# Earlier transposes in the first and the fourth slot of a decoder layer's schedule

## The chip, the cores and the metric

The kernel runs on one core of a Trainium2 chip. The metric is the device time of one execution in microseconds. TensorE (PE in the profile) multiplies matrices and transposes, VectorE (DVE) and ScalarE (ACT) work on elements, GpSimd (POOL) does element work in SBUF only, SyncE (SP) issues DMAs. Matmul results land in PSUM, which has eight banks.

## The reference, cut to what matters

One decoder layer on x of 32 batches, 256 tokens, 256 features, in float32: self attention with 16 query heads and 4 key/value heads of size 64 (rotary positions, a linear position bias), cross attention to a context of the same size with 16 heads of size 16 in windows of 64 with a mask by cell, and a gated feed-forward of 1024 features with quantized weights and activations. After each, the residual is added and a layer norm follows.

```python
x = _layernorm(x + self_attention(x))             # 16 heads, softmax over all 256 keys
x = _layernorm(x + cross_attention(x, ctx, cell)) # own layer norms, windows, mask, softmax
x = _layernorm(x + feed_forward(x))               # down(silu(gate(x)) * up(x)), quantized
```

## The kernel before, in words

All 32 batches go through one software pipeline. Time is cut into **slots**; four slots make a **round** (`m, part = divmod(slot, 4)`), and a batch takes four rounds, sixteen slots. In each round one quarter of a batch's self attention and one quarter of another batch's cross attention are worked on; cross attention runs four rounds behind (`k = m - CROSS`).

A self-attention round has two units. For each unit `self_scores` (L392 on TensorE) makes scores in two PSUM banks `s`, and VectorE adds the position bias and takes each row's maximum, `nm` (L408). `self_exp` (L426, ScalarE) takes the exponentials, two for each half, and their sums. `self_turn` transposes them (`t`, L453) and ScalarE copies them to SBUF as `pT` (L458). In the next round `self_values` multiplies by v (`o`, L470) and ScalarE copies the result to `oT` (L477). `self_inverse` takes the reciprocals of the sums and spreads them (L439, L441, VectorE); `self_spread` transposes them into bank `R` (L485); `self_normal` multiplies `oT` by `R` (L493, VectorE).

A cross-attention round has one unit: `cross_scores` (`xs`, L662, four banks; maxima `xnm` L676 on VectorE), `cross_exp` (L692), `cross_turn` (`xt`, L701; ScalarE copies to `xpT`, L703), `cross_values` (`xo`, L717; copy `xoT`, L726) and `cross_back` (`xr`, L737; `on`, L743).

All else is written as generators with `yield n` for "go on n slots later", and one call `parts()` per slot runs those that are due: `self_inputs` (projections `proj` L329, `psin` L338, `v`, the addition `qT` L353 on GpSimd after a turned copy by DMA), `self_output` (`wo` L501, residual L511 to L528, `zqT` and `zT` L203/L204, `xq` L538, `qb` L556), `cross_inputs` (`zcT`, `xk` L610, `xv` L622, `xvaug` L630), `cross_output` (`zoT`, `xw` L763, L767) and `feed_forward` (`ff` L804 with a tanh L818 and a product L819 for the gate, L825 for up; `ffo` L851; the final norm's `y` and the store of the output). Some operations of ScalarE are kept in the list `last` and come at the end of the slot, in `flush()`.

What sets the order: TensorE, VectorE and ScalarE execute in exactly the order in which the slots record their instructions (`manual_schedule`). GpSimd and SyncE are ordered by the planner of the language, from the recorded program. All PSUM tiles come from one pool of eight banks that are handed out in turn, so a tile gets the bank of the tile eight allocations earlier and waits for its last reader:

```python
ps = ctx.enter_context(tc.tile_pool(name="ps", bufs=8, space=bass.MemoryType.PSUM))
```

Of the kernel before, what the change touches and what calls it, by code (L numbers as in the profile page):

```python
# [50 lines left out]
def kernel(  # L51
# [139 lines left out]
    def flush():  # L191
        while last:
            last.pop(0)()
# [694 lines left out]
    with tc.manual_schedule(engines={mybir.EngineType.PE, mybir.EngineType.DVE, mybir.EngineType.Activation}):  # L888
        running = []
        slot = min(starts)  # L890
        while starts or running:
            m, part = divmod(slot, 4)
            k = m - CROSS
            for gen in starts.pop(slot, ()):
                running.append([slot, gen])

            def cross(f, unit, *more):
                if 0 <= unit < 4 * B:
                    f(*divmod(unit, 4), *more)

            def pair(f, unit):
                if 0 <= unit < 4 * B:
                    f(*divmod(unit, 4))

            def own(f, unit, *more):
                if 0 <= unit < 8 * B:
                    f(*divmod(unit, 8), *more)

            def parts():
                for r in list(running):  # L910
                    if r[0] == slot:
                        wait = next(r[1], r)
                        if wait is r:
                            running.remove(r)
                        else:
                            r[0] += wait or 1

            if part == 0:
                own(self_scores, 2 * m)
                own(self_scores, 2 * m + 1)  # L920
                own(self_exp, 2 * m, 0)
                own(self_exp, 2 * m, 1)
                own(self_exp, 2 * m + 1, 0)
                pair(self_values, m - 1)
                own(self_exp, 2 * m + 1, 1)
                pair(self_spread, m - 1)
                parts()
                pair(self_normal, m - 1)
                cross(cross_turn, k - 1, 0)
                cross(cross_turn, k - 1, 1)  # L930
            elif part == 1:
                parts()
                cross(cross_scores, k)
                cross(cross_values, k - 1)
                cross(cross_exp, k, 0)
            elif part == 2:
                parts()
                cross(cross_exp, k, 1)
                own(self_turn, 2 * m)
                cross(cross_back, k - 1)  # L940
            else:
                pair(self_inverse, m)
                parts()
                own(self_turn, 2 * m + 1)
            flush()
            slot += 1

# [88 lines left out]
```

## Time and profile before

| | us |
|---|---|
| median of 3 runs | 2231.85 (2231.59 to 2232.89) |
| the profiled execution's own time | 2230.19 |
| its span | 2228.4 |
| TensorE busy | 2148.1 (96%) |
| VectorE busy | 1740.1 (78%) |
| ScalarE busy | 1678.0 (75%) |
| GpSimd busy | 1106.4 (50%) |
| mean granted clock of TensorE | 0.986 |

From 140 us to 2030 us every stretch of 70 us has TensorE busy for over 69 us at a granted clock of 1.00; the rest is a start of some 100 us and an end of some 130 us. How to read rows in order of time: start and length in us, engine, line, operation, written tile <- read tiles, their sizes, the number of instructions merged into the row, and in brackets how long the engine stood idle before it and who ended that. Matmuls are pipelined, so the length of a row of TensorE contains about 0.15 us that lie under the next row; the steps from start to start show the pace. In the list of waits the columns are the engine, what waited, for whom, and us in total, times, longest.

### The profile page before, as it was taken

The numbers are of one execution on the slowest core, as the hardware profiler recorded it, in microseconds if no ns is written. First come the engines' busy times: TensorE is split into PE (matmuls) and PEld (weight loads), VectorE is DVE, ScalarE is ACT, GpSimd is POOL, SyncE is SP. The second block draws the span as 40 slices with busy tenths as digits, with TensorE's granted clock in tenths as the row PEclk, the third lists the DMA queues.
The fourth block names the chain that finished last, engine by engine and source line by source line (L and its number), as shares of the span: only waits on it lengthen the run. The fifth ranks groups of instructions, "written<-read, shape, count | busy, mean of one in ns | idle before, by whom it ended". The sixth has DMA issues, their size and how long they took to land.

```text
span 2228.4 us, 55216 instructions
## 1 busy us (share of the span) xinstructions
PE 2148.1 (96%) x17828; PEld 1672.0 (75%) x17828; DVE 1740.1 (78%) x6949; ACT 1678.0 (75%) x4961; POOL 1106.4 (50%) x1849
## 2 busy tenths in 40 slices
PE   7899999999999999999999999999999999999974
PEld 5687777777777777777777777777777777777752
DVE  4777888878887877887877887887788887888775
ACT  2577778887778877778787777887877887777862
POOL 4344554545554545544545544545555445555442
PEclk8999999999999999999999999999999999999996
DMA  6322222222222223222222322222222222222111
GB/s 206 94 57 56 69 55 63 62 56 70 70 54 62 64 55 73 68 57 63 61 58 70 69 59 58 60 64 65 70 66 53 66 58 63 70 63 49 34 41 31
DMA packets 191424, 144.05 MB, mean 65 GB/s; under 512 B 107808, under 2 KB 160928, under 8 KB 191136
## 3 DMA queue, kind: packets, MB, share of 16 engines
q1 hardware_dynamic: 189440, 136.95, 24.6%
q8 instruction: 142, 2.33, 0.5%
q10 hardware_dynamic: 1696, 3.57, 0.4%
q14 instruction: 146, 1.20, 0.2%
HBM read 39.50 MB, written 8.39 MB: 21 GB/s over the span
## 4 chain that ended last, share of the span: by engine, by line
PE 72%; DVE 11%; ACT 9%; issue 3%; DMA 2%; POOL 1%; SPq 1%; ACTq 0%; DVEq 0%; POOLq 0%
PE wo L501 10%; PE o L470 9%; PE proj L329 8%; PE t L453 8%; PE s L392 6%; PE ff L804 5%; ACT p L426 4%; PE xt L701 4%; PE xo L717 3%; PE xq L538 3%; PE xs L662 3%; PE ffo L851 3%; PE R L485 3%; PE xk L610 3%; PE xw L763 2%
## 5 line engine op out<-in xcount | busy, mean ns | idle before, releaser
L426 ACT ACTIVATE p<-p,nm 128x256 f32<-128x256 f32 x1024 | 507.3, 497 | 89.5 <-DVE nm L408 89.5
L458 ACT COPY pT<-t 128x512 f32<-128x512 f32 x512 | 275.9, 597 | 149.0 <-PE t L453 148.3
L408 DVE CUSTOM_DVE_ANT_0 p<-s,alibi 128x256 f32<-128x256 f32 x1024 | 361.9, 417 | 5.0 <-PE s L392 4.9
L692 ACT ACTIVATE xp<-xp,xnm 128x128 f32<-128x128 f32 x1024 | 327.2, 397 | 25.7 <-DVE xnm L676 25.7
L676 DVE CUSTOM_DVE_ANT_0 xp<-xs,mask 128x128 f32<-128x128 f32 x1024 | 225.8, 286 | 82.4 <-PE xs L662 82.1
L453 PE MATMUL t<-ident,p 128*128 128x128 f32 x2048 | 266.8, 273 | 0.9 <-ACT p L426 0.9
L470 PE MATMUL o<-pT,v 128*64 128x256 f32 x2048 | 261.0, 386 | 3.9 <-ACT pT L458 0.9
L453 PEld LDWEIGHTS t<-ident,p 128*128 128x128 f32 x2048 | 238.0, 141 | 27.0 <-ACT p L426 2.6
L353 POOL TENSOR_TENSOR qT<-qT,other 128x512 f32<-128x512 f32 x128 | 163.8, 1279 | 188.4 <-DMA other<-psin 138.7
L392 PE MATMUL s<-kT,qT 64*128 64x256 f32 x2048 | 255.7, 389 | 0.0
L329 PE MATMUL proj<-xT,wq_sb 128*128 128x256 f32 x1024 | 246.4, 385 | 0.0
L501 PE MATMUL wo<-wo_sb,oT 128*128 128x256 f32 x1024 | 245.3, 383 | 0.0
L470 PEld LDWEIGHTS o<-pT,v 128*64 128x64 f32 x2048 | 144.3, 136 | 106.7 <-issue 21.2
L392 PEld LDWEIGHTS s<-kT,qT 64*128 64x128 f32 x2048 | 187.9, 186 | 38.0 <-issue 16.1
L501 PEld LDWEIGHTS wo<-wo_sb,oT 128*128 128x128 f32 x1024 | 191.5, 192 | 27.0 <-DVE gu L297 0.3
L329 PEld LDWEIGHTS proj<-xT,wq_sb 128*128 128x128 f32 x1024 | 188.1, 193 | 21.7
L426 ACT ACTIVATION_READ_ACCUMULATOR p<-p,nm 128x1 f32 x1024 | 192.4, 188 | 0.0
L493 DVE TENSOR_TENSOR oT<-oT,R 128x512 f32<-128x512 f32 x128 | 86.9, 679 | 114.2 <-ACT oT L477 104.2
L840 POOL TENSOR_SCALAR gu<-gu,ffhup 128x1024 f32<-128x1024 f32 x64 | 72.8, 1137 | 161.3 <-DVE ffhup L836 161.3
L819 DVE SCALAR_TENSOR_TENSOR gu<-gu,ff 128x512 f32<-128x512 f32 x128 | 82.5, 684 | 77.2 <-ACT gu L818 77.2
L726 ACT COPY xoT<-xo 128x256 f32<-128x256 f32 x128 | 47.6, 372 | 124.9 <-PE xo L717 123.3
L600 POOL TENSOR_SCALAR mask<-ck_i,cq_sb 64x128 f32<-64x128 f32 (+1 forms) x96 | 70.2, 731 | 141.3 <-DVE xnm L676 135.3
(148 smaller groups left out, 4579.9 us busy)
## 6 DMA issues: line engine op xcount, KB each, us to landing
other<-psin SPq DMA_DIRECT2D x640, 64.0 KB, 2.0
xT<-in_xt_dram SPq DMA_DIRECT2D x32, 256.0 KB, 2.7
xs<-in_x_dram SPq DMA_DIRECT2D x32, 256.0 KB, 2.7
cs<-in_ctx_dram SPq DMA_DIRECT2D x32, 256.0 KB, 2.9
other<-qb SPq DMA_DIRECT2D x64, 128.0 KB, 2.0
kTz<-tr SPq DMA_DIRECT2D x256, 32.0 KB, 2.0
other<-qb SPq DMA_DIRECT2D x128, 64.0 KB, 1.9
out_dram<-x SPq DMA_DIRECT2D x32, 256.0 KB, 2.3
```

What stands on the lines that cost most here:

```text
L329: nc.tensor.matmul(pq[:, c * L : (c + 1) * L], w[:, dc, c * P : (c + 1) * P], xT[:, dc, :], start=(dc == 0), stop=(dc == NDC - 1),)
L353: nc.gpsimd.tensor_tensor(d2, d2, other, ALU.add)
L392: nc.tensor.matmul(banks[half][:, rr * L : (rr + 1) * L], qT[rows_, rr, qc * P : (qc + 1) * P], kT[rows_, kc, :], start=(rr == 0), stop=(r ...
L408: nc.vector.tensor_tensor_reduce(p[:, cols], banks[half][:, cols], alibi[:, 2 * (4 * kc + 2 * rp + rr) + half, :], -0.125, 3.0e38, ALU.add ...
L426: nc.scalar.activation(p[:, cols], p[:, cols], AF.Exp, bias=nm[:, rr : rr + 1], scale=-1.0, accum_out=s["sums", i // 2][:, e : e + 1],)
L453: nc.tensor.transpose(pt[:, j * P : (j + 1) * P], p[half][:, rr * L + kk * P : rr * L + (kk + 1) * P], ident,)
L458: nc.scalar.copy(pT[half], pt)
L470: nc.tensor.matmul(po[half * HD : (half + 1) * HD, rp * L : (rp + 1) * L], s["v"][:, kk, (2 * kc + half) * HD : (2 * kc + half + 1) * HD], ...
L501: nc.tensor.matmul(py[:, 0:D], s["oT", qc, kc][:, r, :], wo_sb[:, 4 * kc + r, :], start=(kc == 0 and r == 0), stop=(kc == 1 and r == 3),)
L676: nc.vector.tensor_tensor_reduce(p[:, cols], banks[2 * half + j // 2][:, j % 2 * P : (j % 2 + 1) * P], s["mask"][:, qc, :], -1.0, 3.0e38, ...
L692: nc.scalar.activation(p[:, cols], p[:, cols], AF.Exp, bias=s["xnm", i][half][:, j : j + 1], scale=-1.0)
L804: nc.tensor.matmul(pg, xiT[:, t, dc, :], ff_w[name][:, dc, half * 512 : (half + 1) * 512], start=(dc == 0), stop=(dc == NDC - 1),)
```

## The change

In a round's first slot `self_spread` and both calls of `cross_turn` are recorded directly behind `self_values`, ahead of the last pair of exponentials (`self_exp(2m+1, 1)`), of the slot's parts and of `self_normal`. In its fourth slot the transposes of the second unit are recorded ahead of the slot's parts.

```diff
             if part == 0:
...
                 own(self_exp, 2 * m + 1, 0)
                 pair(self_values, m - 1)
+                pair(self_spread, m - 1)
+                cross(cross_turn, k - 1, 0)
+                cross(cross_turn, k - 1, 1)
                 own(self_exp, 2 * m + 1, 1)
-                pair(self_spread, m - 1)
                 parts()
                 pair(self_normal, m - 1)
-                cross(cross_turn, k - 1, 0)
-                cross(cross_turn, k - 1, 1)
...
             else:
                 pair(self_inverse, m)
+                own(self_turn, 2 * m + 1)
                 parts()
-                own(self_turn, 2 * m + 1)
             flush()
```

In the built program the instructions are the same in number and kind. On TensorE `xt` (8 transposes) stands directly behind `R`, ahead of `zqT`, `xw` and the other parts of the first slot; `t` of the second unit stands ahead of the fourth slot's parts (gate, up, projection, or projection and `xv`). On ScalarE the two `xpT` copies stand between `oT` and the last two exponentials, and the second pair of `pT` copies ahead of the fourth slot's parts. VectorE's order is unchanged. On SyncE's queue the store of the output moves from behind the DMA transposes of `xiT` to ahead of the four `psin` copies that precede these. On GpSimd the addition L528 moves ahead of three small operations of `rstd_zo`.

## The prediction

> **What bounds the kernel now.** I read the engine shares first, then TensorE's groups in order of time over one batch in mid-run, then ScalarE and VectorE in the same microseconds, then the waits.
>
> ```profile
> PE 2148.1 (96%) x17828; PEld 1672.0 (75%) x17828; DVE 1740.1 (78%) x6949; ACT 1678.0 (75%) x4961; POOL 1106.4 (50%) x1849
> ```
>
> TensorE sets the time, but "96% busy" hides its stalls, since a matmul that waits halfway through a group counts as a longer group. So I look at the step from the start of one group to the start of the next. A batch repeats every 66.4 us (the start of xo at 1004.01, and six batches on at 1402.48). It has four rounds, which I call A to D by where the scores s start: A at 995.64, B at 1009.85, C at 1025.02, D at 1040.19. TensorE in order of time:
>
> ```profile
> 1002.85 0.82 PE L662 MATMUL xs<-kTz,xqT 32*64 32x256 f32 x16
> 1004.01 0.91 PE L717 MATMUL xo<-xpT,xvaug 128*32 128x64 f32 x32 [0.34 <-ACT xpT L703]
> 1004.85 1.16 PE L538 MATMUL xq<-zT,xq_w 128*128 128x128 f32 x8
> ...
> 1009.85 2.00 PE L392 MATMUL s<-kT,qT 64*128 64x256 f32 x16
> 1011.96 2.33 PE L470 MATMUL o<-pT,v 128*64 128x256 f32 x16
> 1014.22 0.66 PE L485 MATMUL R<-ident,wide 128*128 128x128 f32 x4
> ...
> 1018.27 0.71 PE L662 MATMUL xs<-kTz,xqT 32*128 32x256 f32 x8
> 1018.91 0.65 PE L717 MATMUL xo<-xpT,xvaug 128*32 128x64 f32 x32
> ```
>
> Two steps are long. Place (a), round A: xs to xo takes 1.16 where the same shape takes 0.61 in round D (1051.09 to 1051.70), and xo to xq 0.84 where xo takes 0.58: 0.81 us lost. Place (b), the start of round B: s to o 2.11 instead of 1.93, o to R 2.26 instead of 1.88 (both from round C): 0.56 lost. All other steps of the batch are at their usual pace, so some 1.37 us per batch is all that a better order can win back. ScalarE in the same stretch:
>
> ```profile
> 1001.67 0.56 ACT L477 COPY oT<-o 128x512 f32<-128x512 f32 x1
> ...
> 1003.13 0.35 ACT L204 COPY zT<-zqT 128x256 f32<-128x256 f32 x1
> 1003.38 1.06 ACT L703 COPY xpT<-xt 128x512 f32<-128x512 f32 x2
> ...
> 1009.51 1.09 ACT L458 COPY pT<-t 128x512 f32<-128x512 f32 x2
> 1010.45 1.31 ACT L818 ACTIVATE gu<-ff,ffg 128x512 f32<-128x512 f32 x2
> 1011.60 1.12 ACT L458 COPY pT<-t 128x512 f32<-128x512 f32 x2
> 1012.94 0.51 ACT L426 ACTIVATE p<-p,nm 128x256 f32<-128x256 f32 x1 [0.22 <-DVE nm L408]
> ```
>
> ScalarE runs without a gap worth naming from 998.70 to 1012.7; there it, and not TensorE, paces the core. At (a) the two xpT copies end at 1004.44, and xo waits for both. At (b) two things are late: the second pair of pT copies, and a PSUM bank. The waits and VectorE's rows name the bank:
>
> ```profile
> PEld xo L717 <- ACT xpT L703: 44.5, 99, 1.5
> PEld o L470 <- DVE gu L819: 14.7, 29, 0.5
> 1011.22 1.28 DVE L819 SCALAR_TENSOR_TENSOR gu<-gu,ff 128x512 f32<-128x512 f32 x2 [0.50 <-ACT gu L818]
> 1012.42 0.42 DVE L408 CUSTOM_DVE_ANT_0 p<-s,alibi 128x256 f32<-128x256 f32 x1
> ```
>
> The eight banks go round in turn; o is the eighth bank after the first gate bank (gate, gate, t, t, four of s, o), so it starts when L819 has read that one (11.22 + 0.70 = 11.92, o at 11.96). There are 29 such waits: 29 times a gate is followed by a round of scores. (a) looks the same near 272, 538, 738 and 1402 us, each with a 0.33 to 0.34 gap.
>
> **The change, part by part.** No instruction is added or removed; only orders differ. The reciprocal transposes R (L485) were already directly behind o on TensorE: nothing moves there.
>
> *First slot, cross transposes.* On ScalarE the two xpT copies go ahead of the last two exponentials (L426). oT starts at 1001.67 and holds the engine 0.46 (next start 1002.13). The copies hold it 0.95 (1003.38 to 1004.33), so the second ends at about 1003.19; xo is due at 1002.85 + 0.61 = 1003.46 and no longer waits. But the exponentials (1.00, from 1002.13 to 1003.13) now stand ahead of the zT copy: 1003.09 + 1.00 + 0.35 = 1004.44. xq, due at 1003.46 + 0.58 = 1004.04, reads zT and starts about 1004.49 (0.05 behind, as xo was). Before: 1004.85. So the wait moves from xo to xq and of 0.81 only 0.36 is won. Rounds B and D have no zT there, and in C xq starts at 1033.46 against a zT at about 1032.65: nothing. The delayed exponentials are read two slots later by t, covered by 4 us.
>
> On TensorE xt (0.87) goes ahead of zqT or xw. In A zqT is ready (L526 ends 998.26). In D, xw ends 0.87 later, so L767 moves from 1045.55 to about 1046.4, ends its statistics near 1047.4, and L493 starts at 1047.67 anyway because of oT: covered, by 0.3 us.
>
> *Fourth slot, t ahead of the parts.* t (0.87) goes ahead of gate (A), up (B), a projection (C), projection and xv (D). A: pT copies precede the two tanh (L818). xoT can start 0.16 earlier, as xo ends earlier, so ScalarE's stream runs 0.16 ahead: pT(first) 1009.35, pT(second) 1010.30, tanh from 1011.25 to 1012.5. s would start at 1009.85 - 0.36 = 1009.49; its second bank is that of the first pT copy, which ends 9.35 + 0.59 = 9.94, while s wants it two matmuls in (9.73): 0.25 lost anew. s then ends 9.98 + 1.69 = 11.67. The bank of o is now that of the third pT copy (about 10.9) and the last pT is there at 11.4, so neither holds o: R at 11.67 + 1.88 = 13.55, before 14.22. **0.67 won per batch at this point**; I use 0.65.
>
> What does it put late? tanh and L819 come after pT, and VectorE does L819 ahead of the maxima of s (L408). The second tanh ends near 12.55 instead of 11.76, L819 near 13.3; the maxima start at about 13.24 instead of 12.42, 0.82 late. Exponentials 13.76, six at 0.495 to 16.73, oT to 17.29, L493 17.35 to 18.0, which frees the fourth bank of xs (R's). xs starts at 18.27 - 0.65 = 17.62 and asks for that bank 0.48 later, 18.10. Covered, with a tenth to spare; behind that each microsecond costs one. xo's two copies end at 17.19 + 0.95 + 0.10 = 18.24, and xo is due at 17.62 + 0.64 = 18.26: covered, only because they too now precede the exponentials. ScalarE's 1.23 us of idle at 1019.64 takes the rest.
>
> D: psin (L338) needs the projection, 0.87 later: 1057.71 + 0.87 + 1.73 + 0.16 = 1060.47, and VectorE, filled since wo, reaches it at 1060.75. xv's second half ends 1062.2, needed 1062.3. Cover 0.1 to 0.3. B: up needed by 1024.45, ready 1024.0 - 0.65. C: psin 1041.56, ready 1040.25.
>
> *Queues.* On SP the output store (0.53 to issue, 256 KB) passes the four psin copies, the two xvaug copies and the two xiT transposes. It waits for the second y on ScalarE, about 1060.4, so is issued by 61.0; the psin copies behind it start at 61.49 after L338. If y came later, psin would be late, then qT on POOL; POOL idles 4.67 us after that qT. On POOL the x1 bias add passes three short rstd_zo operations; its input is ready at 1061.1 and POOL gets there at 1064.6. Both nothing.
>
> *A rule.* The Trainium skill, "Perfetto Trace Analysis", Identifying Performance Opportunities, Optimization Strategy, says that a bubble repeated on the saturated engine can mean too few SBUF or PSUM buffers for the next tile. The change adds no bank, so by that rule (b) stays: 29 x 0.36 = 10 us won. The rows say that the bank lacks only because of who reads it last (L819 at 11.92 against a pT copy at about 10.9): I go by the rows.
>
> *Tail.* At 2138.80 o waits 0.87 for a pT behind two tanh, and xt (2152.77) stands behind a zqT that waited 2.67: about 1 us each at most, 1.5 taken (0 to 2.5). The first two batches have no gate: nothing.
>
> **Sum.** 29 x 0.65 = 18.9, + 1.5 = 20.4. The profiled execution took 2230.19 (span 2228.4): 2209.8. The median of the runs is 1.66 above it: 2211.5, so **2212 us**. About 0.2% (4.5 us) is what a measurement of this kernel can tell from no change.
>
> **Rivals.**
> *Half of it* (0.14). Only one of the places pays, through xq's wait on zT or the covers of a tenth eating the rest: 0.25 to 0.4 per batch, 7 to 12 us: 2222. For it: both new waits (zT, pT) are my own findings. Against: the xpT and pT copies do come 1.2 us earlier.
> *ScalarE is the bound, nothing moves* (0.09). Its work from 998.70 to 1012.7 is the same sum. Against: what TensorE needs from it is moved ahead of what it doesn't. 2232.
> *All of it* (0.05). zT and pT turn out in time: 29 x 1.37 = 40: 2192.
> *Slower* (0.14). The maxima of round B: the cover is a tenth. If they start at 1014.2 rather than 1013.24, L493 ends 0.96 later, xs stalls 0.9, more than the 0.65: 29 x 0.28 = 8: 2240. It decides from 1013.95 on. For it: VectorE and ScalarE hand over four times in a row there. Against: the tanh can't be later than one pair of copies, 0.95.
>
> **Chances and range.** The main case has 0.58, 2204 to 2219 alone. With half (0.14) and no change (0.09) the range 2204 to 2232 holds 0.81. Faster 0.58 + 0.14 + 0.05 = 0.77; same 0.09; slower 0.14.
>
> **What would show it.** Right: xs to xo 0.61, a new wait of xq for zT near 0.4, o at pace 1.88 with no wait on L819, the maxima of round B some 0.8 later against s than before. Wrong: xs in round B waiting for L493 or oT, s waiting for pT by over 0.3, psin late behind the projection.

## The result, and the profile after

| | us |
|---|---|
| kernel before, median of 4 runs | 2231.72 (2230.14 to 2232.89) |
| changed kernel, median of 4 runs | 2205.71 (2202.09 to 2208.47) |
| ratio, with its 95% interval | 0.9883 (0.9866 to 0.9900) |
| profiled execution: before, after | 2230.19, 2208.47 |

The change wins 26 us by the medians; 20 were forecast. Profile against profile it wins 21.7, and takes 2208.47 where the sum gave 2209.8. That is nearly exact for the profiled execution, which is the longest of the four runs, but in part by luck: two errors cancelled in it, as shown below.

The engine shares of the page after:

```profile
PE 2127.6 (96%) x17766; PEld 1658.8 (75%) x17828; DVE 1742.3 (79%) x6949; ACT 1660.3 (75%) x4961; POOL 1107.7 (50%) x1849
```

TensorE is still "96% busy", and its busy time fell with the span: the row of shares cannot show a stall that hides inside a group of matmuls. The order of time can show it. TensorE, changed kernel; the columns are start and length in us, engine, line, operation:

```profile
993.51 1.25 PE L662 MATMUL xs<-kTz,xqT 32*64 32x256 f32 x16
...
1000.81 2.10 PE L392 MATMUL s<-kT,qT 64*128 64x256 f32 x16
1002.85 1.95 PE L470 MATMUL o<-pT,v 128*64 128x256 f32 x16
1004.73 0.66 PE L485 MATMUL R<-ident,wide 128*128 128x128 f32 x4
...
1008.78 0.71 PE L662 MATMUL xs<-kTz,xqT 32*128 32x256 f32 x8
1009.42 0.65 PE L717 MATMUL xo<-xpT,xvaug 128*32 128x64 f32 x32
...
1059.86 0.69 PE L662 MATMUL xs<-kTz,xqT 32*64 32x256 f32 x16
1060.47 0.65 PE L717 MATMUL xo<-xpT,xvaug 128*32 128x64 f32 x32
1061.49 1.16 PE L538 MATMUL xq<-zT,xq_w 128*128 128x128 f32 x8 [0.36 <-ACT zT L204]
```

Place (a), in round A, is here at 1059.86: xs to xo takes 0.61 (before: 1.16), and then xq waits for zT, so xo to xq takes 1.02 (0.84). Place (b) is the start of round B, at 1000.81: s to o takes 2.04 (2.11), o to R 1.88 (2.26). Round B's xs and xo, at 1008.78 and 1009.42, still run at pace. The first row is the same xs in another batch, with a stall of 0.6 us that the change has not removed; more on it below.

ScalarE, changed kernel:

```profile
1000.67 2.04 ACT L458 COPY pT<-t 128x512 f32<-128x512 f32 x4
1002.56 1.31 ACT L818 ACTIVATE gu<-ff,ffg 128x512 f32<-128x512 f32 x2
1005.05 0.51 ACT L426 ACTIVATE p<-p,nm 128x256 f32<-128x256 f32 x1 [1.18 <-DVE nm L408]
...
1059.13 1.06 ACT L703 COPY xpT<-xt 128x512 f32<-128x512 f32 x2
1060.08 0.52 ACT L426 ACTIVATE p<-p,nm 128x256 f32<-128x256 f32 x1
...
1061.08 0.36 ACT L204 COPY zT<-zqT 128x256 f32<-128x256 f32 x1
```

All four pT copies now come in one row, ahead of the two tanh. In exchange ScalarE stands idle for 1.18 us before round B's exponentials. They start 4.24 us after s (1005.05 against 1000.81); before it was 3.09 (1012.94 against 1009.85). The zT copy stands behind two exponentials, which is what xq waits for. VectorE shows who is late before the exponentials:

```profile
1003.33 1.29 DVE L819 SCALAR_TENSOR_TENSOR gu<-gu,ff 128x512 f32<-128x512 f32 x2 [1.39 <-ACT gu L818]
1004.53 0.42 DVE L408 CUSTOM_DVE_ANT_0 p<-s,alibi 128x256 f32<-128x256 f32 x1
```

The maxima L408 stand behind the gate's two products, and these behind the tanh. In the list of waits of the changed kernel (us in total, times, longest) the same changes are seen as sums:

```profile
ACT p L426 <- DVE nm L408: 241.8, 95, 22.8
PEld xq L538 <- ACT zT L204: 19.5, 34, 1.3
PEld xo L717 <- ACT xpT L703: 12.8, 36, 1.4
```

The wait of o for L819 (14.7 us, 29 times) is gone from the list; the wait of xo for xpT fell from 44.5 to 12.8; the wait of xq for zT, 19.5 now and 0.5 before, is new; and ScalarE's wait for the maxima rose from 89.5 to 241.8.

**Where the 21.7 us between the two profiled executions are.** I took the start-to-start steps of TensorE in all batches between 300 and 1950 us of each trace and, for each step, the median over the batches with the commonest order of groups (21 of 25 before, 19 of 24 after). Only these differ by more than the 0.1 us that the moved groups pass to one another:

| step, us | before | after |
|---|---|---|
| A: xs to xo | 1.16 | 0.62 |
| A: xo to xq | 0.84 | 1.02 |
| B: s to o | 2.10 | 2.03 |
| B: o to R | 2.26 | 1.88 |
| B: xs to xo | 0.64 | 0.64 |
| B: xo to the next | 0.59 | 0.59 |
| sum of a batch's steps | 66.48 | 65.64 |

Some 0.81 to 0.84 are won in a typical batch. The mean over the 27 batches in mid-run is 66.47 before and 65.77 after, 0.70 apart: some batches win less. 27 x 0.70 = 18.9 of the 21.7 us; 2.3 more lie behind the last v (197.87 to 195.55), and some 0.5 in the start. The other 4.3 us of the 26 are in no trace, since only one execution of each kernel was profiled. The start is one candidate: up to v of the fifth batch the ten traces of this case take from 231.2 to 235.8 us, and these two are the two longest.

### The profile page after: what moved, and what is told of

Its sections match the earlier page's. It is cut to its first block, busy times and chain, and to the rows that moved or that the text cites. A ratio compares the mean times of both kernels' runs of the same rounds, so it can differ in the third digit from the quotient of the medians.

```text
span 2206.7 us, 55094 instructions
## 1 busy us (share of the span) xinstructions
PE 2127.6 (96%) x17766; PEld 1658.8 (75%) x17828; DVE 1742.3 (79%) x6949; ACT 1660.3 (75%) x4961; POOL 1107.7 (50%) x1849
## 4 chain that ended last, share of the span: by engine, by line
PE 77%; ACT 8%; DVE 8%; DMA 2%; issue 2%; POOL 1%; SPq 0%; ACTq 0%; POOLq 0%; DVEq 0%
PE wo L501 10%; PE proj L329 10%; PE t L453 10%; PE s L392 8%; PE o L470 8%; ACT p L426 5%; PE ff L804 4%; PE xt L701 4%; PE xq L538 3%; PE xs L662 3%; PE ffo L851 3%; PE xk L610 3%; PE xv L622 2%; PE R L485 2%; PE xw L763 2%; PE v L361 2%
## 5 line engine op out<-in xcount | busy, mean ns | idle before, releaser
L426 ACT ACTIVATE p<-p,nm 128x256 f32<-128x256 f32 x1024 | 508.3, 499 | 241.8 <-DVE nm L408 241.8
L408 DVE CUSTOM_DVE_ANT_0 p<-s,alibi 128x256 f32<-128x256 f32 x1024 | 361.6, 416 | 3.2 <-PE s L392 3.2
L692 ACT ACTIVATE xp<-xp,xnm 128x128 f32<-128x128 f32 x1024 | 328.5, 401 | 33.8 <-DVE xnm L676 33.8
L458 ACT COPY pT<-t 128x512 f32<-128x512 f32 x512 | 263.9, 598 | 9.4 <-PE t L453 9.2
L353 POOL TENSOR_TENSOR qT<-qT,other 128x512 f32<-128x512 f32 x128 | 163.2, 1275 | 182.8 <-DMA other<-psin 100.5
L470 PE MATMUL o<-pT,v 128*64 128x256 f32 x2048 | 250.3, 386 | 0.4 <-ACT pT L458 0.4
L470 PEld LDWEIGHTS o<-pT,v 128*64 128x64 f32 x2048 | 136.0, 136 | 99.2 <-issue 31.1
L493 DVE TENSOR_TENSOR oT<-oT,R 128x512 f32<-128x512 f32 x128 | 87.9, 687 | 104.5 <-ACT oT L477 102.8
L819 DVE SCALAR_TENSOR_TENSOR gu<-gu,ff 128x512 f32<-128x512 f32 x128 | 82.3, 684 | 96.4 <-ACT gu L818 96.4
L703 ACT COPY xpT<-xt 128x512 f32<-128x512 f32 x256 | 135.5, 579 | 0.8 <-PE xt L701 0.7
```

The source lines that it names most:

```text
L353: nc.gpsimd.tensor_tensor(d2, d2, other, ALU.add)
L408: nc.vector.tensor_tensor_reduce(p[:, cols], banks[half][:, cols], alibi[:, 2 * (4 * kc + 2 * rp + rr) + half, :], -0.125, 3.0e38, ALU.add ...
L426: nc.scalar.activation(p[:, cols], p[:, cols], AF.Exp, bias=nm[:, rr : rr + 1], scale=-1.0, accum_out=s["sums", i // 2][:, e : e + 1],)
L458: nc.scalar.copy(pT[half], pt)
L470: nc.tensor.matmul(po[half * HD : (half + 1) * HD, rp * L : (rp + 1) * L], s["v"][:, kk, (2 * kc + half) * HD : (2 * kc + half + 1) * HD], ...
L692: nc.scalar.activation(p[:, cols], p[:, cols], AF.Exp, bias=s["xnm", i][half][:, j : j + 1], scale=-1.0)
```

## The experiments

*Theory.* ScalarE's fixed order decides: what TensorE needs next must come first, and round B's chain (tanh, product L819, maxima, exponentials, oT) then has just enough cover. *Rivals.* One of the two moves pays alone; the new waits of xq and s are what is left to win; the bank of o (its last reader L819), and not the pT copies, held o before.

All kernels below do the full computation. Their times, with the ratio to the kernel before in the same series (its median there was 2232.84 for the first four and 2232.23 for the others):

| kernel | median, us | ratio (95%) |
|---|---|---|
| first slot's move alone | 2224.68 | 0.9964 (0.9950 to 0.9978) |
| fourth slot's move alone | 2241.38 | 1.0043 (1.0028 to 1.0058) |
| changed, parts ahead of the last exponentials | 2206.44 | 0.9883 (0.9868 to 0.9898) |
| the same, pT ahead of xp's exponentials | 2205.08 | 0.9880 (0.9866 to 0.9895) |
| before, second gate product at the slot's end | 2239.91 | 1.0033 (1.0019 to 1.0046) |
| changed, maxima of round B held back | 2223.02 | 0.9955 (0.9940 to 0.9970) |
| changed, parts and pT ahead, xp's second half in the fourth slot | 2192.06 | 0.9814 (0.9799 to 0.9828) |
| changed, xp's second half in the fourth slot, nothing else | 2202.65 | 0.9864 (0.9848 to 0.9881) |

### First slot's move alone

The changed kernel with its fourth slot as before:

```diff
                 pair(self_inverse, m)
-                own(self_turn, 2 * m + 1)
                 parts()
+                own(self_turn, 2 * m + 1)
```

> The first-slot move alone. Theory (ScalarE's order decides, and its total work paces the stretch): xq starts about 0.36 us earlier in each of 29 batches, but at place (b) o still waits for L819 on the gate bank, whose tanh comes only 0.16 us earlier, so 0.16 x 29 = 5 us stay: about 2227 us. Rival (the two places add up independently): 0.36 x 29 = 10 us, about 2221 us.

Measured: 2224.68, 8.2 us won, between the two. TensorE of this kernel:

```profile
1000.79 1.16 PE L538 MATMUL xq<-zT,xq_w 128*128 128x128 f32 x8 [0.47 <-ACT zT L204]
...
1005.79 2.10 PE L392 MATMUL s<-kT,qT 64*128 64x256 f32 x16
1008.07 2.32 PE L470 MATMUL o<-pT,v 128*64 128x256 f32 x16 [0.18 <-DVE gu L819]
```

Place (a) is as in the changed kernel (0.62 and 1.02 by the medians), with the wait of xq for zT. Place (b) is unmended: s to o is even longer, 2.29, since TensorE now arrives there earlier and waits for the same things. The batch is 66.32 in the typical case (66.48 before), so about half of the 0.36 us that (a) should win is lost again 5 us later. The mid-run batches of the trace win 0.17 each, 27 x 0.17 = 4.6 us, which is the theory's 5; the rest of the 8.2 us is not in them. What (a) wins is worth little while ScalarE, late at (b), paces the core.

### Fourth slot's move alone

The kernel before with its fourth slot as in the changed kernel:

```diff
                 pair(self_inverse, m)
+                own(self_turn, 2 * m + 1)
                 parts()
-                own(self_turn, 2 * m + 1)
```

> The fourth-slot move alone. Theory: place (b) is won whole, 0.56 us x 29 = 16 us and about 1 us in the tail, with xo's wait for xpT at place (a) as before: about 2215 us, more than half of the full change. Rival (the copies ahead of the exponentials bring the gain): 5 to 8 us, about 2225 us.

Measured: 2241.38, 8.5 us slower than before. Both expectations fell, with their sign. TensorE of this kernel (PEld is its loading of weights), then its ScalarE:

```profile
1013.89 1.95 PE L470 MATMUL o<-pT,v 128*64 128x256 f32 x16
1015.77 0.66 PE L485 MATMUL R<-ident,wide 128*128 128x128 f32 x4
...
1019.82 0.71 PE L662 MATMUL xs<-kTz,xqT 32*128 32x256 f32 x8
1021.06 0.91 PE L717 MATMUL xo<-xpT,xvaug 128*32 128x64 f32 x32 [0.53 <-DVE xnm L676]
1021.06 0.27 PEld L717 LDWEIGHTS xo<-xpT,xvaug 128*32 128x32 f32 x16 [0.93 <-ACT xpT L703]
```

```profile
1016.02 0.51 ACT L426 ACTIVATE p<-p,nm 128x256 f32<-128x256 f32 x1 [1.18 <-DVE nm L408]
...
1019.45 0.51 ACT L426 ACTIVATE p<-p,nm 128x256 f32<-128x256 f32 x1
...
1020.45 1.04 ACT L703 COPY xpT<-xt 128x512 f32<-128x512 f32 x2
```

Place (b) is won whole: s to o 1.93, o to R 1.88, 0.56 us. But round B now loses 0.86 where nothing was lost before: xs to xo 1.24 and xo to the next group 0.85 (0.64 and 0.59). The ScalarE rows give the reason. The exponentials start 4.06 us after s (1011.96), the last two still precede the xpT copies, and so the first of the two copies starts at 1020.45 and ends at 1021.01, where xo was due at 1019.82 + 0.64 = 1020.46. The row of the matmuls puts xo's wait down to "xnm", but that ended at 1021.07, when xo had begun. The row of its weights names xpT, and they were loaded 0.05 us after the end of that copy.

So the two moves do not add up: 8.2 won and 8.5 lost alone, 26 won together. The first slot's move is the cover of the fourth slot's. The prediction had said so in one clause ("covered, only because they too now precede the exponentials"); my expectation of 2215 for this kernel left it out and was a slip against my own text.

### Parts ahead of the last exponentials

The changed kernel, the zT copy ahead of two exponentials:

```diff
                 cross(cross_turn, k - 1, 1)
-                own(self_exp, 2 * m + 1, 1)
                 parts()
+                own(self_exp, 2 * m + 1, 1)
```

> The changed kernel with the first slot's parts recorded ahead of the last two exponentials, so that the zT copy goes ahead of them on ScalarE. xq's wait for zT (0.44 us) must go. Theory (ScalarE's total work paces the stretch up to the pT copies): s then waits for the first pT copy instead, and the time stays within 3 us of the changed kernel, 2203 to 2206 us. Rival (the wait for zT is a loss of its own): 0.44 x 29 = 13 us less, about 2193 us.

Measured: 2206.44, no difference from the changed kernel, as the theory had it. xq waits no more (xo to xq 0.59), but TensorE loses it again before o. TensorE of this kernel, with the transposes of the second unit, gate and s:

```profile
997.41 1.04 PE L453 MATMUL t<-ident,p 128*128 128x128 f32 x8
998.52 1.02 PE L804 MATMUL ff<-ff_gate,xiT 128*128 128x512 bf16 x4
999.48 2.42 PE L392 MATMUL s<-kT,qT 64*128 64x256 f32 x16
1001.82 1.95 PE L470 MATMUL o<-pT,v 128*64 128x256 f32 x16
```

s to o is 2.34 instead of 2.03, and t to gate 1.11 here (1.00 by the medians, 0.87 after). The weights for which s stands still are loaded at 1000.76, 0.05 us after the end of the second pT copy (the expectation named the first). So from round A's exponentials to s of round B ScalarE holds TensorE, and a wait that is taken away at the start of that stretch comes back at its end.

### Also pT ahead of xp's exponentials

The former kernel, with the third slot's second half of `cross_exp` (four exponentials L692, 1.18 us from start to next start) behind the first unit's pT copies:

```diff
-                cross(cross_exp, k, 1)
                 own(self_turn, 2 * m)
+                cross(cross_exp, k, 1)
```

> As the one with zT ahead, and in the third slot the first pair of pT copies goes ahead of the four cross exponentials as well. Theory: now what TensorE needs next comes first at both places, so both remaining waits (0.44 for zT, 0.1 for pT) go: 0.54 x 29 = 16 us less than the changed kernel, about 2190 us. Rival (the cover in round B is used up, L493 frees the bank of xs too late): no gain, 2203 to 2208 us.

Measured: 2205.08; the theory's 2190 fell and the rival's time came true. s to o is 1.93 now, no wait is left at (a) or (b), and yet the batch takes 65.61: round B's xs to xo takes 0.90 (0.64) and xo to the next 0.70 (0.59). With (a) and (b) cleared, s of round B starts earlier, while tanh, product and maxima do not. TensorE is then held at round B's xs: of its first four matmuls three start from 1005.05 to 1005.06, and the fourth at 1005.32, 0.05 us after the end of oT. That is the third link of the same chain, though not through L493, as the rival had it.

### The bank of o alone

The kernel before, with the gate's second tanh and product L819 at the slot's end, behind the pT copies:

```diff
-                nc.scalar.activation(cols, pg, AF.Tanh, scale=g_of[:, t : t + 1])
-                nc.vector.scalar_tensor_tensor(cols, cols, 1.0, pg, ALU.add, ALU.mult)
+                def gated(cols=cols, pg=pg, t=t):
+                    nc.scalar.activation(cols, pg, AF.Tanh, scale=g_of[:, t : t + 1])
+                    nc.vector.scalar_tensor_tensor(cols, cols, 1.0, pg, ALU.add, ALU.mult)
+                if t:
+                    last.append(gated)
+                else:
+                    gated()
```

> The kernel before, with the gate's second pair of tanh and of products (L818, L819) kept back to the end of the slot: TensorE's order and so the banks are as before (o takes the first gate bank), but the pT copies go ahead of the tanh. Theory (the bank and its last reader hold o at place (b)): o waits for an L819 that is now about 0.9 us later, round B's o starts near 0.9 us later and runs at its usual pace, 0.53 us x 29 = 15 us lost, about 2247 us. Rival (the order of the pT copies alone held o): 0.5 us x 29 = 15 us won, about 2217 us.

Measured: 2239.91, slower as the theory said, but not in its place. TensorE and VectorE of this kernel:

```profile
1013.75 1.95 PE L470 MATMUL o<-pT,v 128*64 128x256 f32 x16
...
1020.93 0.91 PE L717 MATMUL xo<-xpT,xvaug 128*32 128x64 f32 x32 [0.53 <-DVE xnm L676]
```

```profile
1014.16 1.28 DVE L821 SCALAR_TENSOR_TENSOR gu<-gu,ff 128x512 f32<-128x512 f32 x2 [1.48 <-ACT gu L820]
```

o starts at 1013.75, before the product (here L821) begins at 1014.16. So o does not wait for it, and s to o and o to R are at pace (1.93, 1.88). The loss is the one of the fourth slot's move: round B's xs to xo 1.25 and xo to the next 0.84. The bank numbers in the built programs tell why o is free. The pool does not hand out its banks in a fixed round. A new tile gets the bank that was released first in the recorded order. Before, o of round B has the first gate bank, as I had read from the times; with the product recorded later, the first bank to be released is a t bank, and o gets that one. In the changed kernel it is a t bank as well. So this kernel tried the order of ScalarE once more, and the bank not alone. How much of (b)'s 0.56 us was the bank and how much the pT copies can be read from the kernel before, in its loading of weights:

```profile
1011.96 0.62 PEld L470 LDWEIGHTS o<-pT,v 128*64 128x64 f32 x6 [0.51 <-DVE gu L819]
1012.77 1.06 PEld L470 LDWEIGHTS o<-pT,v 128*64 128x64 f32 x10 [0.19 <-ACT pT L458]
```

o began when L819 had freed its bank, but one of its two halves then stood still until the fourth pT copy had ended (1012.72), and from 1012.77 it ran at its pace to the end. All 29 such groups show the same two waits. With a free bank o would have begun at an estimated 1011.78 (1009.85 + 1.93) and met the same copy. So by the order of time the copy alone held R at 1014.22, and the wait for the bank lay in front of a longer one. A kernel with another bank and the old order of copies was not run.

### Maxima of round B held back

The changed kernel with an unused maximum of 128 x 512 elements on VectorE, ahead of round B's maxima:

```diff
                 nc.vector.scalar_tensor_tensor(cols, cols, 1.0, pg, ALU.add, ALU.mult)
+            if t:
+                nc.vector.tensor_reduce(small("spare", 1), rs_sb, AX.XY, ALU.max)
```

> The changed kernel with one more operation on VectorE per gate (a maximum over 128 x 512, some 0.65 us, its result unused) directly ahead of round B's maxima. Theory (round B has a cover of a tenth; behind it each us of late maxima comes back through the exponentials, oT, L493 and the fourth bank of xs): xs or xo in round B 0.5 to 0.65 us longer, 29 x 0.6 = 17 us, about 2223 us. Rival (there is cover left): within 3 us of the changed kernel, about 2206 us.

Measured: 2223.02, as the theory had it, and 17.3 us above the changed kernel. VectorE and TensorE of this kernel:

```profile
1009.72 0.68 DVE L821 TENSOR_REDUCE spare<-rs_sb 128x1 f32<-128x512 f32 x1
1010.32 0.41 DVE L408 CUSTOM_DVE_ANT_0 p<-s,alibi 128x256 f32<-128x256 f32 x1
```

```profile
1013.96 1.14 PE L662 MATMUL xs<-kTz,xqT 32*128 32x256 f32 x8
1015.03 0.77 PE L717 MATMUL xo<-xpT,xvaug 128*32 128x64 f32 x32
1015.74 1.04 PE L804 MATMUL ff<-ff_up,xiT 128*128 128x512 bf16 x3
```

The maxima start 0.60 us late (1009.72 to 1010.32), and xs to xo takes 1.07 and xo to the next 0.71: 0.55 lost in a batch. 17.3 us over 29 gates is 0.60. So there is next to no cover left in the changed kernel: what makes these maxima later costs nearly its whole length. By the bank numbers the fourth bank of this xs is that of o, which the oT copy releases, and the third that of xw, released by L767. L767 ended at 1013.48, before xs began. Of the first four matmuls of xs, one for each bank, three start from 1013.96 to 1013.98 and the fourth at 1014.41, 0.05 us after the end of oT (1014.36). xo then waits for its second xpT copy, which ended at 1015.32; the weights that need it were loaded at 1015.37.

### Round B's chain relieved

If that chain is the last link, then 1.18 us of ScalarE's work that stands ahead of it should go into the 1.18 us in which ScalarE waits for the maxima. The kernel with both waits cleared, and the second half of `cross_exp` at the end of the fourth slot:

```diff
             elif part == 2:
                 parts()
                 own(self_turn, 2 * m)
-                cross(cross_exp, k, 1)
+                if m >= 4 * B:
+                    cross(cross_exp, k, 1)
                 cross(cross_back, k - 1)
             else:
                 pair(self_inverse, m)
                 own(self_turn, 2 * m + 1)
                 parts()
+                if m < 4 * B:
+                    cross(cross_exp, k, 1)
```

The conditions keep the old place in the last rounds, which have no self attention.

> zT ahead of the last exponentials, the first pT pair ahead of the cross exponentials, and the second half of the cross exponentials (four, 1.18 us) at the end of the fourth slot, behind pT and tanh, where ScalarE stood idle for 1.18 us before round B's exponentials. Theory (round B's chain of maxima, exponentials, oT, L493, bank of xs is what is left): its tanh and maxima come 1.2 us earlier, xs and xo lose nothing in round B, xq nothing in round A: 65.2 to 65.3 us per batch instead of 65.65, 0.35 to 0.45 x 29 = 10 to 13 us less than the changed kernel, about 2194 us. Rival (ScalarE's sum of work is the limit): 2203 to 2207 us.

Measured: 2192.06, 13.7 us below the changed kernel, with a ratio to the kernel before of 0.9814 (0.9799 to 0.9828). It beats both kernels. ScalarE of this kernel, and TensorE:

```profile
990.40 2.08 ACT L458 COPY pT<-t 128x512 f32<-128x512 f32 x4
992.31 1.34 ACT L818 ACTIVATE gu<-ff,ffg 128x512 f32<-128x512 f32 x2
993.46 1.34 ACT L692 ACTIVATE xp<-xp,xnm 128x128 f32<-128x128 f32 x4
994.82 0.51 ACT L426 ACTIVATE p<-p,nm 128x256 f32<-128x256 f32 x1
```

```profile
985.07 0.69 PE L662 MATMUL xs<-kTz,xqT 32*64 32x256 f32 x16
985.69 0.65 PE L717 MATMUL xo<-xpT,xvaug 128*32 128x64 f32 x32
986.27 1.16 PE L538 MATMUL xq<-zT,xq_w 128*128 128x128 f32 x8
...
991.42 2.00 PE L392 MATMUL s<-kT,qT 64*128 64x256 f32 x16
993.35 1.95 PE L470 MATMUL o<-pT,v 128*64 128x256 f32 x16
995.23 0.66 PE L485 MATMUL R<-ident,wide 128*128 128x128 f32 x4
```

The four exponentials of xp lie between the tanh and the maxima's arrival, ScalarE runs without a gap worth naming, and its exponentials start 3.40 us after s instead of 4.24. TensorE is at pace in (a), in (b) and in round B; of the 1.37 us per batch only 0.16 is left, before the gate (t to gate 1.03, against 0.87). A typical batch takes 65.30, as the theory had it. Of the 15.4 us between the profiled executions of the changed kernel and this one (2193.06), 10.3 lie in the 27 mid-run batches (65.77 and 65.39 on average), and 4.1 up to the fifth v (235.35 and 231.24), where the traces scatter anyway.

### That move alone

The changed kernel with the last edit only:

```diff
-                cross(cross_exp, k, 1)
+                if m >= 4 * B:
+                    cross(cross_exp, k, 1)
...
                 parts()
+                if m < 4 * B:
+                    cross(cross_exp, k, 1)
```

> The changed kernel with only the second half of the cross exponentials moved to the end of the fourth slot. Theory: s no longer waits for pT (0.1 us), xq still waits for zT (0.44 us): 3 us less than the changed kernel, about 2203 us. Rival (the late maxima were the real limit and zT no loss of its own): as the one with zT ahead too, about 2194 us.

Measured: 2202.65, 3.1 us below the changed kernel. s no longer waits for pT (s to o 1.93), but xq still waits for zT (xo to xq 1.03), and a typical batch takes 65.57. Once more the parts do not add up: clearing xq's and s's waits wins 0.6 us, which is no difference beside the spread of the runs, this move 3.1, where the intervals of the two ratios still overlap, and both together 13.7.

## Why the prediction was right, and where it was not

- **What bounds the kernel** (TensorE, with ScalarE pacing it from 998.70 to 1012.7): right, and its consequence was wider than I wrote. The moves have to be judged along that whole stretch and not place by place.
- **Place (a)**, 0.36 of 0.81 won, the wait going from xo to xq: right. The medians give 0.54 won at xo and 0.18 lost at xq, 0.36 in sum; xq waits 0.36 to 0.47.
- **Place (b)**, "0.25 lost anew" by s waiting for the first pT copy: the mis-sized term. s to o is 2.03 where 1.93 is its pace, so 0.10 is lost, and a typical batch wins 0.81 to 0.84 instead of 0.65. What failed is the rule of the banks in turn. By the bank numbers of the built program the first pT copy frees the third bank of s and not the second, and the second copy the fourth; s loads the weights for these two 0.76 us after its start and not 0.24. The first copy (end 1001.26) came in time. The weights that wait for the second (end 1001.74) were loaded at 1001.79 instead of 1001.57.
- **The maxima of round B, 0.82 later**: right in size. By the sum they were to start at 13.24 with s at 9.49, 3.75 us after it; they start 3.72 after it (1004.53 against 1000.81), where it was 2.57 before. "Behind that each microsecond costs one": the held maxima confirm it, 0.60 us later and 0.60 us per gate lost. That round B is covered at all was luck as far as xs goes, for two errors cancel there. The fourth bank of xs is not R's, released by L493, but that of o, freed by the copy oT; and xs asks for all four banks within 0.02 us, not for the last one 0.48 later. oT ended at 1008.58, and the fourth matmul started on time at 1008.80. L493 ended at 1009.30: had xs needed that, round B would have lost an estimated 0.5 us (1009.30 - 1008.80). The tightest link is the one that the sum had right, xo's copies (18.24 against 18.26): the second ended at 1009.54, and the weights that need it were loaded on time at 1009.62. Weights follow such a copy by 0.05 at the least in these traces, so 0.03 is left.
- **Eight banks "in turn"**, as the text before the prediction has it too: wrong. A tile gets the bank that was released first. For o both rules give the same bank, the gate's before the change and that of the third pT copy after it; for s and xs in round B they don't, which is where the two terms above went wrong. The bank was also not what held o before: its wait lay in front of the one for the fourth pT copy.
- **Round D**, "cover 0.1 to 0.3" for xv: used up, without harm. `xvaug` waits 0.22 to 0.44 us for xv (8.5 us in 31 waits; before, 0.9 in 2), but the operation behind it, L793, ends no later for it. What the sum left out are irregular batches: in five of the 27, as in the one whose xs at 993.51 takes 1.25, round A's exponentials start later (there 3.72 us after s instead of 3.05), and xs and xo lose 0.30 to 0.67, some 2.1 us in all, or 0.08 of the 0.12 per batch by which the mean gain is below the typical one. The rows are a long L793 and a regular one, each with the operation of GpSimd beside it:

```profile
986.75 1.27 POOL L573 TENSOR_TENSOR other<-other,rx_sb 128x512 f32<-128x512 f32 x1
987.08 1.22 DVE L793 TENSOR_SCALAR xib<-tr 128x512 bf16<-128x512 f32 x1
...
1052.43 1.27 POOL L573 TENSOR_TENSOR other<-other,rx_sb 128x512 f32<-128x512 f32 x1
1053.42 0.56 DVE L793 TENSOR_SCALAR xib<-tr 128x512 bf16<-128x512 f32 x1
```

L793 ends 0.28 us after GpSimd's operation, both times. GpSimd is late in just these five batches: its addition qT (L353), which waits for the DMA of `psin`, starts 6.15 to 6.50 us before s there and 6.95 to 8.01 in the others, but for one that is irregular elsewhere. Why that DMA is late stays open; the kernel before has such late additions too, so the change did not bring them.

- **The tail**, 1.5 (0 to 2.5): 2.3 behind the last v, and 0.5 in the start, for which I had 0. In the one wait of o for pT, 0.87 became 0.4.
- **Queues**: right. The output store is issued at 1050.88 and the psin copies from 1052.00; L528's place shows nowhere.
- **The rule** of the Trainium skill ("Perfetto Trace Analysis", Identifying Performance Opportunities, Optimization Strategy), by which a repeated bubble can mean too few buffers: it did not apply here. No bank was added and the bubble at (b) is gone, o to R 1.88. By the rule 10 us would have been won. The page says "can mean", and the bank was indeed waited for (14.7 us in 29 waits); but behind that wait stood a longer one, for a copy.

The sum of 29 x 0.65 was met by 27 x 0.70, and the profiled execution by 1.3 us. That closeness is luck: s's wait was taken 0.15 too long, and the irregular batches, 0.12, were not in it. Of the rivals, "half of it" did not come: both places pay, (a) 0.36 and (b) 0.45. "Slower" is what the fourth slot's move does without the first's, by another link than the one I named: xo's wait for xpT and not the bank of xs. "All of it" (2192) was nearly to be had, as the last kernel but one shows (1.18 of the 1.37 us in a typical batch), but not by this change.

## What to carry to other kernels

When a second engine with a fixed order paces the first, cost a reordering along the whole stretch that it paces: follow the chain from the work that was moved back to the next time that the bounding engine asks for it, and ask there what the cover was. Two moves of which one loses 8.5 us and one wins 8.2 can win 26 together, so a move that loses alone is not yet a bad one. And after a move, look for the idle time that it made on the second engine: here 1.18 us ahead of the exponentials, which was just the room for another 1.18 us of its work, and worth some 13 us once the two other waits were cleared.

## What was not expected of the hardware

- A group of matmuls does not stand still as a whole. s goes in pairs, one matmul for each half of the array's rows. In the changed kernel one half keeps its pace of 0.22 us (starts at 1001.57, 1001.78, 1002.00, 1002.21, 1002.43), while the other, whose weights came 0.22 late, starts at 1001.57, 1001.79, 1002.11, 1002.33, 1002.54: of the 0.22 only 0.10 is lost.
- The same VectorE operation on the same shape (L793, 128x512 to bf16) took 0.56 us in one batch and 1.22 in another of the same execution. In all 27 mid-run batches of the kernel before, and in all 27 of the changed one, it took what the running operation of GpSimd still had to go (0.17 to 1.04 us), plus 0.28 to 0.30. No run moved GpSimd's operation away.
- A matmul's wait can have another name than that of its weights. In the fourth slot's move alone the row of xo's matmuls says "xnm" (0.53 us), which ended when they had begun; the row of their weights says xpT, which is right by the order of time.
